# A two-layer graph attention kernel: second layer's tiles cleared earlier in shared memory, transposes three units ahead instead of four, norms over five slots instead of eight

## The chip, the cores and the metric

The kernel runs on one core of one Trainium2 chip. Times are device microseconds of one execution. The engines that appear below are PE (TensorE, matrix products and transposes), PEld (its weight loads), DVE (VectorE), ACT (ScalarE), POOL (GpSimd, which here also issues the gathers), SP (SyncE, which issues most of the other transfers).

## The reference

Two graph attention layers over the same graph, then a norm, the residual and a second norm. B = 8 batches, N = 2048 nodes, 64 channels, H = 4 heads in the first layer and one in the second.

```python
mask = graph + jnp.eye(N, dtype=graph.dtype) > 0
h = jnp.einsum('bnc,hdc->bhnd', x, Wh)
out_h = _gat_layer(h, mask[None, None], bh[None, :, None, :])   # softmax(mask(h h^T)) h + b
z = jax.nn.leaky_relu(cat, negative_slope=0.2)                  # cat: the heads side by side
h2 = jnp.einsum('bnk,dk->bnd', z, Wo)
out2 = _gat_layer(h2, mask[None], bo)
z2 = jax.nn.leaky_relu(out2, negative_slope=0.2)
out = (z2 - mu) * jax.lax.rsqrt(var + LN_EPS) * gamma + beta
x = _layernorm(x + out, axis=-1)
```

The graph is sparse and its first nodes have many neighbours.

## The kernel before

**Hubs and sets.** The first 56 nodes (hubs) are attended densely. The other 1992 nodes form NS = 166 sets of 12. For each set the kernel finds up to 128 nodes that any member is linked to, gathers their rows by an indirect transfer from a table in device memory (`gather`, L792, issued by POOL, some 266 KB each), and computes the attention of the 12 members over these 128 rows for all batches at once.

**First layer.** A loop over i from -4 to 85 works on one pair of sets per turn (NG = 83 pairs), software-pipelined: in one turn the scores of pair i + 1, the values of pair i, the projection of pair i - 1 (`project`, L531), the maps into the second layer of pair i - 2 (`second_maps`, L880) and the rows for the second table of pair i - 3 (`second_rows`, L890; `keep_rows`, L894, and its two stores, L897). Tiles of PSUM have the tags "S" (scores), "C" (`cat`), "O" and "T", one buffer of two banks each; `cat` holds the columns, the projection, the maps and the rows of a turn. The memory of the `early` pool is given back when the loop ends.

**Second layer.** It gathers from the second table, which must be complete. Units are u = 0 to 41, of four sets each (NU = 42; the last has two). The loop runs from u = -4 to 48. Turn u of it issues, in this order:

1. `scores2(u + 2)` (L1133 on PE, exponent L1136 on ACT);
2. `values2(u)` (L1165); an odd unit completes a block of 8 sets in PSUM (tag "O", one buffer) and starts its norm;
3. on some turns `hub_values2` (L1299) for the hub block that began two turns earlier, and the load of a later block (`hub_block`, L1267, issued by SP);
4. the four gathers of unit u + 6;
5. the norm's jobs of this turn's first slot (`work_on(u, 0)`), then `roots` (L1239, L1240 on ACT);
6. `hub_lift2` of the hub block of the turn before (L1285 on DVE, L1288 on ACT);
7. `spread_own(u + 3)` (L1124 on ACT): the members' own columns, copied block-diagonally into one of three `bd` tiles, which `scores2` uses as weights;
8. `turn_scores(u + 1)` (L1144 on PE) and `keep_scores(u + 1)` (L1152 on DVE), which masks the exponents into `es2`, the weights of `values2`;
9. `turn2(u + 4)`: 16 transposes of gathered rows (L512 on PE) and two copies to `xTg` (L1320 on ACT);
10. `hub_scores2` (L1277 on PE);
11. the norm's jobs of the second slot (`work_on(u, 1)`).

The transposes and the hub's scores share the PSUM tag "T" with two buffers. There are 18 hub blocks: four in turns -4 to -1, the others in turns 2, 4, ..., 28.

**The norm** of a block of 8 sets is a list of jobs, spread over turns: `first` (reciprocals L1186 and product L1188), `act` (L1193), `mean` (L1197), `centre` (L1202 on DVE and the square L1204 on ACT), `var` (L1213), `again` (L1217, L1221, L1222: scale, gamma, residual row `xr`), a second `mean`, `centre` and `var`, and `end` (scale L1217 and eight stores L1248). Each turn's list has a part for slot 0 and a part for slot 1:

```python
return [([], [first, act, mean(0)]), ([centre(0)], []), ([var(0)], []), ([], [again, mean(1)]), ([centre(1)], []),
        ([], []), ([var(1)], []), ([end], [])]
```

A new block starts every second turn, so the lists of several blocks overlap. The inverse roots of two variances that fall on one turn are computed together.

**What sets the order.** The schedule is by hand: each engine executes its instructions in the order of the code. Waits between engines come from the tiles: reads after writes, and writes into a tile or buffer after its last reader.

Before the loop of the second layer, and after the first has ended, the code clears `ownb`, `bd`, `es2` and the ends of `esh` (L1107 to L1115), fills `linked` from `mask` (L1117), loads four hub blocks and spreads the first unit.

Of the kernel before, what the change touches and what calls it, by code (L numbers as in the profile page):

```python
# [30 lines left out]
F32 = mybir.dt.float32  # L31
# [13 lines left out]
HUB = 56  # L45
# [314 lines left out]
def fast_kernel(ctx: ExitStack, tc: tile.TileContext, x, adj, Wh, bh, Wo, bo, gamma, beta, out, flag):  # L360
# [53 lines left out]
    nc.vector.tensor_copy(identb, ident)  # L414
    wnat = early.tile([P, H, C], F32, name="wnat")
    whT = early.tile([P, H * D], F32, name="whT")
    gram = early.tile([P, H, P], F32, name="gram")
    wos = early.tile([D, H * D], F32, name="wos")
    woT = early.tile([P, HP, D], F32, name="woT")
# [64 lines left out]
    for k in range(SET):  # L484
        nc.gpsimd.affine_select(out=d, in_=d, pattern=[[0, 3], [-1, 10]], base=-10 * k, channel_multiplier=1,
                                compare_op=OP.not_equal, fill=float(1 << k))
    number = early.tile([P, 2, HALFN], U16, name="number")
    nc.gpsimd.iota(number, [[1, 2], [2, SEG // 2], [SEG, HALFN // (SEG // 2)]], base=0, channel_multiplier=0)
# [20 lines left out]
    def turn(tp, rows):  # L509

        for q in range(Q):
            nc.tensor.transpose(tp[:, q * P:(q + 1) * P], rows[:, q, 1:1 + P], ident)  # L512

# [54 lines left out]

    yh = early.tile([P, 2, 2 * HUB * H], F32, name="yh")

# [91 lines left out]

    keys = [early.tile([P, HALFN], F32, name=f"keys{k}") for k in range(2)]
    cand = early.tile([P, SEG * KEEP], F32, name="cand")
    best = early.tile([P, P], F32, name="best")
    ahead = {}
# [225 lines left out]
    def keep_rows(g, pr):  # L892
        r = rowts[g % 4]
        nc.vector.tensor_tensor(r[:GM, 1:1 + P], pr, bob[:GM].rearrange("n p d -> n (p d)"), OP.add)  # L894
        dst = table2[HUB:, :].rearrange("(n s) (q c) -> s q n c", s=NS, q=Q)
        for j in range(2):
            nc.sync.dma_start(out=dst[2 * g + j], in_=r[j * 48:(j + 1) * 48])  # L897

# [108 lines left out]
    def one(name, tag):  # L1007
        return psum1.tile([P, 2, 512], F32, tag=tag, name=name)

    def late_two(name):  # L1010
        return one(name, "T")

    picks = pick(1)
    ready, done = FIRST, 2 * FIRST
    todo3 = [(10, 0), (14, 1)]
    slow = hub_later(0, one) + hub_later(1, one)
    for i in range(-4, NG + 3):
# [4 lines left out]
        if i >= 1 and slow and len(slow) % 3:  # L1022
            slow.pop(0)()
        cat = one(f"cat{i}", "C")
        if 0 <= i - 1 < NG:
# [14 lines left out]
        if i + 6 < NG and i % 2 == 0 and i >= -2:  # L1040
            own_rows((i + 6) // 2)
        if 0 <= (i - 30) // 2 <= NV:
            (add_beta if i % 2 else load_own)((i - 30) // 2)
# [17 lines left out]
        if 0 <= i - 2 < NG:  # L1061
            second_maps(i - 2, cat[:, 0, 384:384 + GM])
        if 0 <= i - 3 < NG:
            second_rows(i - 3, cat[:GM, 1, 384:512])
        if 0 <= i + 4 < NG + NG % 2:
            columns(i + 4, cat)
        if 0 <= i - 2 < NG:
            keep_own(i - 2, cat[:, 0, 384:384 + GM])
        if 0 <= i - 3 < NG:
            keep_rows(i - 3, cat[:GM, 1, 384:512])  # L1070
        for _ in range((2 if i < 22 or i % 2 else 1) if i >= 0 else 0):
# [10 lines left out]
        if 0 <= i + 3 < NG:  # L1082
            turn(tp[:, 1, :], rows[1, 2 * (i + 3) + 1])
    assert not picks and not pieces and not todo3 and done == NS
    begin.close()
# [11 lines left out]

    NU = (NS + 3) // 4
    sets = [list(range(4 * u, min(4 * u + 4, NS))) for u in range(NU)]
    for u in range(6):  # L1100
        for s in sets[u]:
            gather(table2, s, 2, rows2)
    bd = [late.tile([P, 4, Q, 32], F32, name=f"bd{k}", bufs=1) for k in range(3)]
    es2 = [late.tile([P, 2 * Q, 4, 32], F32, name=f"es2_{k}", bufs=1) for k in range(2)]
    esh = [late.tile([P, Q * 2 * HUB + 8], F32, name=f"esh{k}", bufs=1) for k in range(2)]
    ownb = late.tile([P, Q, 2, HUB], F32, name="ownb", bufs=1)
    nc.vector.memset(ownb, 0.0)  # L1107
    for p in range(2):
        nc.vector.tensor_copy(ownb[half(p), :, p, :], ownh[half(p)].rearrange("c t (k n) -> c (t k) n", k=2))
    for t in bd:  # L1110
        nc.vector.memset(t, 0.0)
    for k in range(2):
        nc.vector.memset(esh[k][:, Q * 2 * HUB:], 1.0)
        nc.vector.memset(es2[k], 0.0)
    nc.vector.memset(es2[0][:, :, :, 24:], 1.0)  # L1115
    linked = late.tile([P, NS, SET], U8, name="linked", bufs=1)
    nc.vector.tensor_scalar(linked, mask.rearrange("p s (k h) -> p s k h", h=H)[:, :, :, 0], 0.0, None, OP.is_equal)  # L1117

    def spread_own(u):

        w = len(sets[u])
        for p in range(2):
            src = own[half(p), :, sets[u][0] * SET:(sets[u][0] + w) * SET]
            nc.scalar.copy(bd[u % 3][half(p), :w, :, 16 * p:16 * p + SET], src.rearrange("c q (k n) -> c k q n", k=w))  # L1124

# [45 lines left out]
    def norm(name, v, i, vals, dens, nb, store):  # L1171

        y = late.tile([P, 8, D], F32, tag="y", name=f"y_{name}", bufs=6)[:, :nb]
        st = late.tile([P, 2, 8], F32, tag="st", name=f"st_{name}", bufs=6)[:, :, :nb]
        at = [v + 2, v + 6]
        xr = late.tile([P, 8, D], F32, tag="xr", name=f"xr_{name}", bufs=3)
# [47 lines left out]
        def end():  # L1224
            scale(1)
            store(y)

        return [([], [first, act, mean(0)]), ([centre(0)], []), ([var(0)], []), ([], [again, mean(1)]), ([centre(1)], []),
                ([], []), ([var(1)], []), ([end], [])]

# [11 lines left out]
    def norm_sets(v, op):  # L1242
        def store(y):
            for t in range(4):
                for a in range(2):
                    dst, w = nodes(t, v)(out, a)
                    p0 = t * 32 + a * SET
                    (nc.scalar if v == NV - 1 and a else nc.sync).dma_start(out=dst, in_=y[p0:p0 + SET].rearrange("p (f w) c -> p f (w c)", f=2)[:, :, :w * D])  # L1248

        view = op[:, :, :4 * W2].rearrange("p f (w c) -> p f w c", w=4)  # L1250
        return norm(f"s{v}", 2 * v + 1, v, view[:, :, :, 1:1 + D], view, 8, store)
# [9 lines left out]

    def hub_block(b):
        t = rows["h", b] = late.tile([P, Q, PW], F32, tag="hrows", name=f"gh{b}", bufs=4)
        n = HUB if b == NHB else hub_sets(b)[1] * SET
        s0 = b * S10
        src = table2[:HUB, :] if b == NHB else table2[HUB:, :].rearrange("(k s) c -> s k c", s=NS)[s0:s0 + n // SET]
        nc.sync.dma_start(out=t.rearrange("n q c -> n (q c)")[:n], in_=src)  # L1267

# [35 lines left out]
    def spread(u, parts):  # L1304

        for k, part in enumerate(parts):
            for t in range(2):
                jobs.setdefault((u + k, t), []).extend(part[t])

# [4 lines left out]
    def turn2(u):  # L1314
        for g in sorted({s // 2 for s in sets[u]}):
            tp = bank2(f"t2_{g}", "T", 2)
            for j in range(2):
                turn(tp[:, j, :], rows[2, 2 * g + j])
            t = held["T", 2, g] = late.tile([P, 2, 512], F32, tag="xTg", name=f"xTg2_{g}", bufs=6)
            nc.scalar.copy(t, tp)  # L1320
# [24 lines left out]

    hub_at = {u: b for b, u in enumerate([-4, -3, -2, -1] + list(range(2, 2 * NHB, 2))[:NHB - 3])}
    assert len(hub_at) == NHB + 1
    for b in range(4):
        hub_block(b)
    spread_own(0)  # L1350
    for u in range(-4, NU + 7):
        if 0 <= u + 2 < NU:
            scores2(u + 2)
        if 0 <= u < NU:
            a = u % 2
            if a == 0:
                op = bank2(f"o2_{u}", "O")
            values2(op, sets[u], es2[a], a, len(sets[u + 1]) if a == 0 else 0)
            if a == 1:
                spread(u, norm_sets(u // 2, op))  # L1360
        if u - 2 in hub_at:
            b = hub_at[u - 2]
            hub_values2(b, b == 0, b == NHB)
            if b + 4 <= NHB:
                hub_block(b + 4)
            if b == NHB:
                spread(u, norm_hub(u, oh2))
        for s in sets[u + 6] if 0 <= u < NU - 6 else []:
            gather(table2, s, 2, rows2)
        work_on(u, 0)  # L1370
        roots(u)
        if u - 1 in hub_at:
            hub_lift2(hub_at[u - 1])
        if 0 <= u + 3 < NU and u > -3:
            spread_own(u + 3)
        if 0 <= u + 1 < NU:
            turn_scores(u + 1)
            a = (u + 1) % 2
            if u + 3 == NU and len(sets[NU - 1]) < 4:

                nc.vector.memset(es2[a][:, :, len(sets[NU - 1]):, SET:2 * SET], 1.0)
            keep_scores(u + 1, a)
        if u + 4 < NU:
            turn2(u + 4)
        if u in hub_at:
            hub_scores2(hub_at[u])
        work_on(u, 1)
        if u == -3:
            range_of(0, rall)
            lists_fit()  # L1390
        if u == NU - 1:
            range_of(1, rall2)
            in_limits()
# [40 lines left out]
```

## Time and profile before

| | us |
|---|---|
| median of three runs | 1047.05 (1044.12 to 1052.09) |
| the profiled execution | 880.76 |
| its span | 878.9 |
| mean granted PE clock in it | 0.951 |

| engine | busy us | share of the span |
|---|---|---|
| PE | 753.0 | 86% |
| PEld | 661.2 | 75% |
| DVE | 610.1 | 69% |
| ACT | 514.4 | 59% |
| POOL | 469.2 | 53% |

Durations below are from the profiled execution, which was shorter than the timed runs. "Idle before <-X" in a row is the time an engine did nothing ahead of an instruction, and what ended it. "issue" is time with no visible cause. An engine's share over the whole span mixes three stages: up to about 600 us the first layer, from there to about 850 us the second, then a tail of norms and stores.

### The profile page before, as it was taken

The page shows a single profiled execution, that of the slowest core. Times are in us where ns is not written, and L with a number is a line of the kernel's source. Part 1 is how long each engine was busy: PE and PEld are TensorE (multiplying, and loading weights), DVE is VectorE, ACT ScalarE, POOL GpSimd, SP SyncE. Part 2 cuts the span into 40 slices and gives each one's busy share as a digit, 9 for nine tenths or more (in the row PEclk, how much of TensorE's full clock was granted, in tenths as well). Part 3 has the DMA queues.
Part 4 walks back from the last instruction along what each step waited for, and adds up shares of the span by engine and source line. Part 5 has one row for each costly group of instructions (what it writes and reads, how often), then busy time and mean ns, then how long its engine had stood idle before and what let it go on. Part 6 is the DMA issues. An engine that isn't in the chain of part 4 may idle for free.

```text
span 878.9 us, 42066 instructions
## 1 busy us (share of the span) xinstructions
PE 753.0 (86%) x18437; PEld 661.2 (75%) x18437; DVE 610.1 (69%) x1369; ACT 514.4 (59%) x961; POOL 469.2 (53%) x612
## 2 busy tenths in 40 slices
PE   1896777889999999999999999992999999998730
PEld 1664456778788999988999999971899999988720
DVE  3356983568888788877555555553258999998994
ACT  2342333556556667666766667651678888886821
POOL 5654141457444555655666666503777777777300
PEclk9998998999999999999999999995999999999965
DMA  8787451355434445655566665514888888888611
GB/s 167 238 218 213 129 146 48 83 142 160 109 100 118 112 125 159 162 169 153 160 168 173 160 166 162 134 28 114 246 266 253 275 275 267 266 252 242 172 46 35
DMA packets 81794, 145.22 MB, mean 165 GB/s; under 512 B 30146, under 2 KB 46466, under 8 KB 81602
## 3 DMA queue, kind: packets, MB, share of 16 engines
q0 software_dynamic: 26720, 88.55, 36.4%
q1 hardware_dynamic: 37842, 49.65, 18.7%
q10 hardware_dynamic: 17040, 4.25, 2.6%
q8 instruction: 147, 2.41, 1.1%
q14 instruction: 45, 0.37, 0.1%
HBM read 123.91 MB, written 18.48 MB: 162 GB/s over the span
## 4 chain that ended last, share of the span: by engine, by line
PE 63%; DVE 15%; DMA 7%; ACT 5%; issue 4%; SPq 3%; POOL 2%; DVEq 0%; ACTq 0%; POOLq 0%
PE t L512 11%; PE s L821 10%; PE o L846 10%; PE cat L806 6%; PE o L863 4%; PE cat L531 4%; PE cat L880 3%; PE s L1133 3%; PE o L1165 3%; PE cat L890 2%; DMA raw<-in_adj_dram 2%; SPq L1248 2%; PE sh L1277 2%; PE e L1144 2%; DMA g<-table,index 1%
## 5 line engine op out<-in xcount | busy, mean ns | idle before, releaser
L792 POOL DMA_INDIRECT g<-table,index x332 | 334.9, 1009 | 236.1 <-PE o L846 140.2
L512 PE MATMUL t<-ident,g 128*128 128x128 f32 x1328 | 182.3, 276 | 15.6 <-DMA g<-table,index 12.7
L512 PEld LDWEIGHTS t<-ident,g 128*128 128x128 f32 x1328 | 154.8, 142 | 20.0 <-issue 14.0
L826 DVE TENSOR_TENSOR e<-s,mask 128x768 f32<-128x768 f32 x83 | 79.4, 956 | 87.4 <-PE s L821 85.4
L518 ACT ACTIVATE z<-cat,bhp 128x192 f32<-128x192 f32 x166 | 60.8, 418 | 85.0 <-PE cat L531 85.0
L846 PE MATMUL o<-g,e 128*64 128x65 f32 x2656 | 97.5, 227 | 0.0
L821 PEld LDWEIGHTS s<-y,xTg 64*64 64x64 f32 x5312 | 85.2, 134 | 13.9 <-issue 13.7
L821 PE MATMUL s<-y,xTg 64*64 64x48 f32 x5312 | 95.5, 220 | 0.0
L846 PEld LDWEIGHTS o<-g,e 128*64 128x64 f32 x2656 | 85.8, 140 | 9.8
L1320 ACT COPY xTg<-t 128x1024 f32<-128x1024 f32 x83 | 80.3, 1017 | 18.1 <-PE t L512 17.3
L1030 ACT COPY xTg<-t 128x1024 f32<-128x1024 f32 x83 | 84.0, 1012 | 2.0 <-PE t L512 2.0
L833 ACT ACTIVATE e<-e,shifts 128x768 f32<-128x768 f32 x83 | 79.2, 955 | 2.1 <-DVE e L826 1.7
L812 ACT COPY y<-cat 128x384 f32<-128x384 f32 (+1 forms) x80 | 40.7, 508 | 64.0 <-PE o L863 40.1
L597 ACT ACTIVATE e<-e,shifts 128x896 f32<-128x896 f32 x32 | 33.4, 1042 | 73.0 <-DVE e L594 52.1
L680 POOL TENSOR_SCALAR a<-raw 120x1024 bf16<-120x1024 int32 (+1 forms) x34 | 38.2, 1125 | 65.1 <-DMA raw<-in_adj_dram 38.4
L806 PE MATMUL cat<-xo,gram 128*128 128x192 f32 (+1 forms) x320 | 65.6, 328 | 0.0
L853 DVE RECIPROCAL rall<-o 64x8 f32<-64x8 f32 x166 | 34.0, 205 | 42.0 <-PE o L846 40.7
L854 DVE TENSOR_TENSOR osb<-o,rall 128x512 f32<-128x512 f32 x83 | 57.4, 692 | 2.9
L1165 PE MATMUL o<-g,es 128*32 128x65 f32 x2656 | 49.1, 226 | 5.9 <-DVE y_s L1188 4.5
L806 PEld LDWEIGHTS cat<-xo,gram 128*128 128x128 f32 x320 | 53.7, 203 | 0.3 <-issue 0.2
L1165 PEld LDWEIGHTS o<-g,es 128*32 128x32 f32 x2656 | 46.1, 113 | 7.0 <-issue 4.9
L1133 PE MATMUL s<-xTg,bd 128*32 128x128 f32 x1328 | 45.4, 277 | 6.2 <-ACT bd L1124 3.5
(177 smaller groups left out, 1369.3 us busy)
## 6 DMA issues: line engine op xcount, KB each, us to landing
raw<-in_adj_dram SPq DMA_DIRECT2D x32, 480.0 KB
table<-xb SPq DMA_DIRECT2D x22, 256.0 KB
xr_s<-table SPq DMA_DIRECT2D x21, 256.0 KB
g<-table,index POOLq DMA_INDIRECT x332
table<-x SPq DMA_DIRECT2D x16, 260.0 KB
x<-in_x_dram ACTq DMA_DIRECT2D x32, 128.0 KB
table<-rowt SPq DMA_DIRECT2D x166, 24.4 KB
xb<-in_x_dram SPq DMA_DIRECT2D x164, 24.0 KB
```

Of the source, the lines that this page charges most:

```text
L512: nc.tensor.transpose(tp[:, q * P:(q + 1) * P], rows[:, q, 1:1 + P], ident)
L518: nc.scalar.activation(z[:, hp], cat[:, :, hp * n:(hp + 1) * n], AF.Identity, bias=bhp[:, hp:hp + 1], scale=1.0)
L792: nc.gpsimd.indirect_dma_start(out=t.rearrange("n q c -> n (q c)"), out_offset=None, in_=table, in_offset=bass.IndirectOffsetOnAxis(ap=ind ...
L806: nc.tensor.matmul(cat[:, k, 2 * GM:2 * GM + n], gram[:, g % 2 * 2 + k, :], held["x", g // 2][:, :n], start=True, stop=True)
L821: nc.tensor.matmul(sp[half(r), p, (q * 2 + j) * M:(q * 2 + j + 1) * M], xt[half(p), j, q, half(r)], y[half(p), (j * Q + q) * M:(j * Q + q ...
L826: nc.vector.tensor_tensor(e[:, :16 * M].rearrange("p (a q n) -> p a q n", a=2, q=Q), sp[:, :, :8 * M].rearrange("p a (q n) -> p a q n", q= ...
L833: nc.scalar.activation(e[:, :16 * M], e[:, :16 * M], AF.Exp, bias=shifts[:, 0:1], scale=1.0)
L846: nc.tensor.matmul(op[half(p), j, o0:o0 + K1], e[:, c0:c0 + 64], rw[j][:, q, sums(p)], start=True, stop=True)
L1030: nc.scalar.copy(t, held.pop(("tp", i + 2)))
L1133: nc.tensor.matmul(sp[q * 32:(q + 1) * 32, k, :], bd[u % 3][:, k, q, :], xt[:, s % 2, q, :], start=True, stop=True, tile_position=(0, q * 32))
L1165: nc.tensor.matmul(op[t * 32:(t + 1) * 32, f, k * W2 + p:k * W2 + p + K1], e[:, 2 * q + p, k, :], rw[:, q, sums(p)], start=(a == 0 and k = ...
L1320: nc.scalar.copy(t, tp)
```

## The change

- The tiles that the second layer clears are no longer allocated at its start. They are views of six tiles `share` in the pool that lives throughout, whose memory first serves helpers of the first layer (`wnat`, `wos`, `number`, `yh`, `keys`, `cand`, `best`). `linked` lies in a part of `maskh`. The clears, `linked` and the first three `spread_own` become eleven jobs, one in every second turn of the first layer's loop from i = 61.
- In the first layer's last turns the maps and the rows have PSUM tiles of their own (from i = 83), and no `cat` is allocated after that turn. In the last two pairs the second store of rows is issued by ACT.
- `turn2` is three units ahead instead of four, and stands right after the norm's first slot. The loop starts at -3. The hub blocks start at turns -3, -2, -1, 2, 4, ..., 30. The first four hub loads wait for transposes of the first units.
- The norm takes five turns instead of eight, `first` ahead of the other jobs of its slot. `roots` comes at the end of the turn. The stores of the last block go over SP, ACT and POOL.

```diff
+    bd = [t.rearrange("p (k q n) -> p k q n", k=4, q=Q) for t in (share[2][:, :512], share[2][:, 512:], share[4])]
+    es2 = [t.rearrange("p (b k n) -> p b k n", b=2 * Q, k=4) for t in share[:2]]
+    ahead_of_second = ([clear_own] + [lambda t=t: nc.vector.memset(t, 0.0) for t in bd + es2] + [clear_ends, link] +
+                       [lambda u=u: spread_own(u) for u in range(3)])
...
-        cat = one(f"cat{i}", "C")
+        cat = one(f"cat{i}", "C") if i <= NG else None
+        if i < NG:
+            ph, pr = cat[:, 0, 384:384 + GM], cat[:GM, 1, 384:512]
+        else:
+            ph, pr = one(f"ph{i}", "S")[:, 0, :GM], one(f"pr{i}", "T")[:GM, 0, :P]
...
+        if i >= 60 and i % 2 and ahead_of_second:
+            ahead_of_second.pop(0)()
...
-            nc.sync.dma_start(out=dst[2 * g + j], in_=r[j * 48:(j + 1) * 48])
+            (nc.scalar if j and g >= NG - 2 else nc.sync).dma_start(out=dst[2 * g + j], in_=r[j * 48:(j + 1) * 48])
...
-        return [([], [first, act, mean(0)]), ([centre(0)], []), ([var(0)], []), ([], [again, mean(1)]), ([centre(1)], []),
-                ([], []), ([var(1)], []), ([end], [])]
+        return [([first], [act]), ([mean(0), centre(0)], [var(0)]), ([again], [mean(1)]), ([centre(1)], [var(1)]), ([], [end])]
...
-                jobs.setdefault((u + k, t), []).extend(part[t])
+                now = jobs.setdefault((u + k, t), [])
+                now[:] = now + part[t] if k else part[t] + now
...
-    for u in range(-4, NU + 7):
+    for u in range(-3, NU + 5):
         if 0 <= u + 2 < NU:
             scores2(u + 2)
         if 0 <= u < NU:
...
+        for s in sets[u + 6] if 0 <= u < NU - 6 else []:
+            gather(table2, s, 2, rows2)
+        work_on(u, 0)
+        if u + 3 < NU:
+            turn2(u + 3)
+        if u in (-3, -2):
+            for k in range(2):
+                hub_block(2 * (u + 3) + k, held["at", 4 * (u + 3) + 2 * k + 1])
         if u - 2 in hub_at:
             b = hub_at[u - 2]
             hub_values2(b, b == 0, b == NHB)
             if b + 4 <= NHB:
                 hub_block(b + 4)
             if b == NHB:
-                spread(u, norm_hub(u, oh2))
-        for s in sets[u + 6] if 0 <= u < NU - 6 else []:
-            gather(table2, s, 2, rows2)
-        work_on(u, 0)
-        roots(u)
+                spread(u + 2, norm_hub(u + 2, oh2))
         if u - 1 in hub_at:
             hub_lift2(hub_at[u - 1])
-        if 0 <= u + 3 < NU and u > -3:
+        if 3 <= u + 3 < NU and u >= 0:
             spread_own(u + 3)
         if 0 <= u + 1 < NU:
             turn_scores(u + 1)
...
-        if u + 4 < NU:
-            turn2(u + 4)
         if u in hub_at:
             hub_scores2(hub_at[u])
         work_on(u, 1)
+        roots(u)
```

The rest moves the definitions up and changes the turns of the final checks (`range_of`) by one.

## The prediction

> **What bounds the kernel now.** I read the engine totals first, then busy time by stretch, then the timeline of one pair of units of the second layer, then the seam between the layers and the tail.
>
> Busy time by stretch (columns: stretch, length, busy and count for PE, PEld, DVE, ACT, POOL, then granted clock, DMA share, GB/s):
>
> ```profile
> 600.00:651.00 51.00, 36.84 (x693) 32.83 (x694) 17.66 (x37) 25.65 (x42) 34.85 (x36) 0.82 0.77 231
> 651.00:788.00 137.00, 134.01 (x3334) 123.94 (x3333) 124.25 (x221) 111.66 (x195) 105.31 (x105) 1.00 0.87 261
> 788.00:850.00 62.00, 45.41 (x1225) 40.68 (x1223) 57.28 (x107) 39.61 (x74) 27.82 (x27) 0.92 0.61 175
> 850.00:879.00 29.00, 0.19 (x2) 0.09 (x2) 16.44 (x32) 4.40 (x12) 0.00 (x0) 0.50 0.15 34
> ```
>
> In the second layer's steady stretch (651 to 788) PE is nearly solid, but DVE is 91% busy and ACT 82%: nobody has room. From 788 on DVE leads; the last 29 us have no PE work.
>
> The timeline of one pair (start, length, engine, line, idle before it). An odd unit begins with its value product at 711.74, the next odd unit at 722.25: period 10.51 us.
>
> ```profile
> 711.74 1.13 PE L1165 MATMUL o<-g,es 128*32 128x65 f32 x64
> ...
> 713.50 0.56 DVE L1152 TENSOR_TENSOR es<-e,linked 128x384 f32<-128x384 f32 x1
> 713.61 0.67 ACT L1288 ACTIVATE esh<-esh,shifts 120x448 f32<-120x448 f32 x1
> 713.97 0.41 DVE L1186 RECIPROCAL rall<-o 64x8 f32<-64x8 f32 x2
> 714.18 0.70 ACT L1124 COPY bd<-own 64x192 f32<-64x192 f32 x2
> ...
> 714.90 1.93 ACT L1320 COPY xTg<-t 128x1024 f32<-128x1024 f32 x2
> 715.14 0.81 PEld L1133 LDWEIGHTS s<-xTg,bd 128*32 128x32 f32 x32 [0.17 <-issue]
> ...
> 717.79 0.63 ACT L1204 ACTIVATE sq_s<-y_s 128x512 f32<-128x512 f32 x1 [0.24 <-DVE y_s L1202]
> ...
> 720.34 1.09 PE L1277 MATMUL sh<-ownb,own 128*120 128x112 f32 x8 [0.23 <-ACT xTg L1320]
> ```
>
> What to see: the scores (L1133) start at 715.14, while the copies of this unit's transposes (L1320) have only just begun. Those copies feed the scores one unit later. This whole unit of slack is why PE loses just 0.23 us a pair although ACT, whose instructions here stand in the order of the code, also waits for DVE (0.24 before the square).
>
> The seam and the tail:
>
> ```profile
> 599.94 0.42 PE L890 MATMUL cat<-ident,own 128*96 128x128 f32 x1 [0.70 <-DVE rowt L894]
> ...
> 605.05 0.43 DVE L1107 MEMSET ownb<- 128x448 f32 x1 [4.36 <-DMA table<-rowt]
> 605.49 0.96 POOL L792 DMA_INDIRECT g<-table,index  x1 [5.56 <-DVE ownb L1107]
> ```
> ```profile
> 633.26 1.09 PE L1165 MATMUL o<-g,es 128*32 128x65 f32 x64
> ```
> ```profile
> 867.92 7.03 SPq L1248 DMA_DIRECT2D out_dram<-y_s  x11
> ```
>
> The first gather goes 5.5 us after the first layer's last product, gathers then follow every 1.25 us (605.49, 606.76, 608.01), and the first value product comes at 633.26, held back by the fourth unit's transposes, that is by the 16th gather. At the end SP still issues stores until 874.95, 0.64 us each, though DVE ended at 869.43.
>
> [...]
>
> **The change, part by part.** The sum is made against the profiled execution, 880.76 us (span 878.9). The median, 1047.05, is 166 us above it; I return to this.
>
> 1. *Clears and block-diagonal copies moved into the first layer.* Eleven jobs, one in every second unit from i = 61: one clear with two copies (0.43 + 0.57), three clears of 0.52, two of 0.91, 0.4 of small ones, `linked` 1.20, three `spread_own` of 0.70 on ACT. The units are 5.00 us long there; DVE shows 1.61 us idle before L826 in each, ACT 0.66 and 0.93. The DVE job delays the copy of `rowt` (530.21 to 530.49 in a unit whose next `cat` product starts at 531.85): slack 1.3 us, the longest job 1.2. I take nothing; without this cover all of it, 6 us of DVE and 2 of ACT, is the upper end. Nothing can be gained within those units.
>
> 2. *Seam.* With `ph` and `pr` in banks of their own, the maps of the last unit no longer wait for `rowt` (597.95 becomes about 597.0, when L523 ends); the last `rowt` ends near 598.8 for 600.69. ACT takes every second store of the last two units, one SP issue of 0.59 each. The gather also no longer sits behind the late pool's clear (605.05 to 605.49). First gather near 602.7: 2.8 us earlier. Transposing three units ahead, the first value product needs the 12th gather and not the 16th: 4 x 1.25 = 5 us. Together **-8** (-5 if half of the seam stays; -10 with the hub loads out of the gathers' way, since SP now issues them after transposes; nothing else is behind them in SP's queue before the first `xr` load).
>
> 3. *Steady state.* No instruction is added, but the order is. Now transposes for u+3 are turned in unit u and needed by the scores at the start of unit u+1: the slack unit is gone. ACT's copies stand behind the squares, and `bd` behind the copies. On DVE an odd unit now has `first` (which waits for this unit's value product) and `again` ahead of the hub subtraction and `keep_scores`; an even unit has `centre(1)`, `mean(0)`, `centre(0)` ahead. The loop, from the start of an odd value product as 0, with starts as they follow each other in the pair above:
>  - DVE: `first` from 1.15 (L1186 0.45, L1188 0.73) to 2.33; `again` 3 x 0.72 to 4.5; hub subtraction 0.54 to 5.05; `keep_scores` 0.47 to 5.5; `act` 0.73, `end` 0.60, `mean(1)` 0.60, `centre(1)` 0.60, `mean(0)` 0.60, `centre(0)` 0.68: 9.33.
>  - ACT: square to 10.0, two copies 1.93 to 11.93, `bd` 0.70 to 12.63.
>  - PE: scores from 12.65, next odd value product 0.89 later: **13.54**, against 10.51.
>
>  Within it, the even unit's scores wait too: hub subtraction 5.1, exponent 0.67, `bd` 0.70: 6.45, where they began at 3.40 before. PE idles about 2 us there and is done with the even unit's transposes at 10.2, ahead of ACT, so the loop above stays the longest. In odd units the hub's score tile still holds one of the two "T" banks, so the second transposes wait for the first copy, about 1.1 us, inside the same idle time. Fifteen periods (odd units 3 to 33) are 15 x 13.54 = 203. After the hub blocks a period is 13.0 (no subtraction); three of them 39; the last, without transposes, 9.6; the hub's norm, some 5 us of small DVE operations, falls into this part: 54. Sum 257. Before, L1188 runs from 651.29 to 851.25: 200.0 for the same 19 periods. **+57**. Bounds: +25 if ACT's squares stand in the way but half of DVE's order overlaps, +70 if odd and even stalls add.
>
> 4. *Drain.* From the last L1186 (850.80) DVE took 18.6 us; in five slots, by the same durations, 17. The stores of the unit before the last now leave some 5 us earlier, the last eight go over three queues: about 2 us of issues for 5.5. **-5.5** (0 to -8).
>
> Sum: 880.8 - 8 + 57 - 5.5 = **924** in the profiled execution, +5%.
>
> *To the median.* The page does not show why the timed runs take 166 us more. If it is a lower PE clock, 753 us of PE work at 0.951 would have to run at about 0.79 (an estimate). Then a pair needs 10.28/0.79 = 13 us of PE before, and in the changed order about 15.4 (the even unit's 5.9 us of PE becomes 7.5 and follows a start at 7.9); 15 x 2.35 + 10 after the hub blocks - 14 = +31. If it is a constant, +43. I take 1047 + 35 = **1082**.
>
> **The rivals.**
> - *The loop does not bind* (ends on the other side). PE's 134 of 137 us and an unchanged number of instructions speak for it: the pair would stay at 10.5, and seam and drain give -13.5: 1033. It needs the DVE-ACT loop to be 3 us shorter than the walk, for example `again` overlapping PE entirely. Against: DVE has 0.64 us idle in a pair and is in order. From a loop below 11.2 us the change gains (0.7 x 19 = 13).
> - *Half of it*: only the even unit's wait for `bd` costs, period 11.2 to 11.5: +13 to +19 against -13.5: 1050.
> - *POOL becomes the pace*: eight gathers of 1.25 are 10.0 us a pair, below 10.5, so it can hold back the early units only; then the seam gains 3 and not 8 while the loop stands: 1087.
> - *The change does not do what it says*: the clears are not covered and the drain stays: 8 + 5.5 more, 1096.
>
> **How the numbers follow.** 0.72 for the loop (1058 to 1112 with the bounds and the last two rivals), 0.12 for half of it (1040 to 1057), 0.16 for no loop (1025 to 1039). A measurement of this kernel tells about 1% from no change. Faster 0.15, within 1% 0.11, slower 0.74. The range 1040 to 1112 leaves out the no-loop case and the far ends of the first.
>
> **What would show it.** Right: in the steady part L1188 to L1188 of neighbouring pairs near 13.5 us; PE's scores L1133 waiting for ACT (`bd` or `xTg`) in both units; ACT's square waiting for DVE, over 1 us; PE's busy share there near 75%; first value product near 625; last DVE to end some 5 us. Wrong: a period at or below 11, or PE waiting in the first layer from i = 61 on.

## The result and the profile after

| | before | after | ratio after to before |
|---|---|---|---|
| first measurement, median of 4 runs each | 1045.59 us | 1108.43 us | 1.0594 [1.0557, 1.0631] |
| both again, medians | 1045.66 us | 1107.86 us | 1.0592 [1.0509, 1.0676] |

The change makes the kernel 5.9% slower. The prediction was 1082 us, with 1040 to 1112 as its range and 0.74 on slower.

The absolute times need one sentence ahead of all that follows: the runs came from several chips, on two of them the kernel before takes 1040 to 1046 us and on two others 881 or 882 us, and the profile of before shown above is like the latter. Where it matters the chip is therefore named by the time of before on it, and runs are compared by their ratio to before on the same chip. The ratio hardly depends on it: 1.0605 [1.0485, 1.0724] for (nearly) the kernel after on a chip of the quick kind.

The engine totals of after, and the shares of its chain of waits (columns as above):

```profile
PE 846.5 (76%) x18437; PEld 719.5 (65%) x18437; DVE 612.9 (55%) x1369; ACT 518.5 (47%) x959; POOL 465.6 (42%) x614
...
PE 58%; DVE 13%; another core or an unknown queue 10%; ACT 8%; issue 5%; DMA 3%; POOL 2%; SPq 0%; ACTq 0%; DVEq 0%; POOLq 0%
```

DVE and ACT do what they did, in a longer span. A tenth of the chain ends on something that the trace does not name. Busy time by stretch, cut where the stages of before were cut (seam, second layer, its end, tail):

```profile
638.00:690.00 52.00, 25.99 (x286) 20.20 (x287) 4.48 (x10) 9.43 (x12) 25.86 (x28) 0.66 0.56 160
690.00:1010.00 320.00, 214.51 (x3948) 178.99 (x3947) 139.91 (x247) 132.08 (x229) 119.30 (x124) 0.82 0.50 135
1010.00:1084.00 74.00, 47.42 (x985) 41.27 (x986) 49.23 (x95) 34.28 (x64) 14.67 (x15) 0.81 0.34 92
1084.00:1110.50 26.50, 1.27 (x34) 0.92 (x34) 15.48 (x30) 3.77 (x10) 1.23 (x2) 0.50 0.16 36
```

In the second layer PE is busy 67% of the time (214.51 of 320), DVE 44%, ACT 41%, and the granted clock is 0.82: nobody is the limit, they wait for each other.

The profile of before that is fit to set beside it is one from the same chip. Both kernels were therefore profiled once more on the chip where before takes 1045.66 us (`b_again`, `a_again`). Cut by the starts of named products (last scores of the first layer, L823; first and last value product of the second, L1180; L821 and L1165 in before), and likewise for the quick chips:

| stage, us | before | after | difference | before, quick chip | after, quick chip (`e4_pad128`) | difference | forecast |
|---|---|---|---|---|---|---|---|
| start to last scores | 613.5 | 619.6 | +6.1 | 584.8 | 589.5 | +4.7 | 0 |
| seam, to the first value product | 66.5 | 62.1 | -4.4 | 48.4 | 39.4 | -9.0 | -8 |
| first to last value product | 320.8 | 398.7 | +77.9 | 213.1 | 274.2 | +61.1 | +57 |
| drain, to the end | 32.3 | 26.2 | -6.1 | 32.5 | 26.8 | -5.7 | -5.5 |
| span | 1033.2 | 1106.6 | +73.4 | 878.9 | 929.9 | +51.0 | +43.5 |

The time is lost in the steady part of the second layer, as forecast; two stages give some back. (The profiled execution of `b_again` took 1035.14 us, 11 less than its median, so the differences on this chip are too large by about as much. The forecast's +57 was made for a stretch that is cut a little differently, from the second block's L1188 to the last one's.)

### The profile page after: what moved, and what is told of

The parts are those of the page before. It is cut to its first block, busy times and chain, and to the rows that moved or that the text cites. A ratio compares the mean times of both kernels' runs of the same rounds, so it can differ in the third digit from the quotient of the medians.

```text
span 1110.5 us, 42062 instructions
## 1 busy us (share of the span) xinstructions
PE 846.5 (76%) x18437; PEld 719.5 (65%) x18437; DVE 612.9 (55%) x1369; ACT 518.5 (47%) x959; POOL 465.6 (42%) x614
## 3 DMA queue, kind: packets, MB, share of 16 engines
q8 instruction: 147, 2.41, 0.9%
## 4 chain that ended last, share of the span: by engine, by line
PE 58%; DVE 13%; another core or an unknown queue 10%; ACT 8%; issue 5%; DMA 3%; POOL 2%; SPq 0%; ACTq 0%; DVEq 0%; POOLq 0%
PE t L513 12%; PE s L823 9%; PE o L848 8%; PE cat L808 4%; PE s L1148 4%; ACT xTg L1340 3%; PE cat L533 3%; PE o L865 3%; PE o L1180 3%; PE e L1159 3%; PE cat L882 2%; PE cat L892 2%; DVE var L1228 2%; DVE e L596 1%
## 5 line engine op out<-in xcount | busy, mean ns | idle before, releaser
L513 PE MATMUL t<-ident,g 128*128 128x128 f32 x1328 | 217.5, 295 | 89.2 <-ACT xTg L1340 56.7
L513 PEld LDWEIGHTS t<-ident,g 128*128 128x128 f32 x1328 | 165.4, 151 | 116.3 <-ACT xTg L1340 60.1
L823 PE MATMUL s<-y,xTg 64*64 64x48 f32 x5312 | 115.1, 222 | 6.4 <-issue 5.7
L823 PEld LDWEIGHTS s<-y,xTg 64*64 64x64 f32 x5312 | 98.8, 134 | 26.4 <-issue 18.5
L1148 PE MATMUL s<-xTg,share 128*32 128x128 f32 x1328 | 61.2, 342 | 58.1 <-ACT share L1028 48.8
L1148 PEld LDWEIGHTS s<-xTg,share 128*32 128x32 f32 x1328 | 44.7, 136 | 71.1 <-ACT share L1028 62.0
L1167 DVE TENSOR_TENSOR share<-e,maskh 128x384 f32<-128x384 f32 (+1 forms) x42 | 23.1, 549 | 116.6 <-PE e L1159 95.5
L1180 PE MATMUL o<-g,share 128*32 128x65 f32 x2656 | 62.4, 264 | 4.4 <-DVE share L1167 4.2
L1180 PEld LDWEIGHTS o<-g,share 128*32 128x32 f32 x2656 | 59.9, 141 | 5.9 <-DVE share L1167 4.8
L1201 DVE RECIPROCAL rall<-o 64x8 f32<-64x8 f32 x42 | 8.6, 205 | 95.9 <-remote 79.6
```

The lines of the kernel that those rows point to most:

```text
L513: at = nc.tensor.transpose(tp[:, q * P:(q + 1) * P], rows[:, q, 1:1 + P], ident)
L823: nc.tensor.matmul(sp[half(r), p, (q * 2 + j) * M:(q * 2 + j + 1) * M], xt[half(p), j, q, half(r)], y[half(p), (j * Q + q) * M:(j * Q + q ...
L1148: nc.tensor.matmul(sp[q * 32:(q + 1) * 32, k, :], bd[u % 3][:, k, q, :], xt[:, s % 2, q, :], start=True, stop=True, tile_position=(0, q * 32))
L1180: nc.tensor.matmul(op[t * 32:(t + 1) * 32, f, k * W2 + p:k * W2 + p + K1], e[:, 2 * q + p, k, :], rw[:, q, sums(p)], start=(a == 0 and k = ...
```

## The experiments

Theory **L** is that of the prediction: PE, ACT and DVE wait for each other in a loop of 13.54 us per pair of units. Two parts of the change are in it: the transposes three units ahead and the norm over five slots (four units long) with its new order.

### Twice the same, and PE's instructions shifted

Because the pair takes about 20.75 us on the chip of the first measurement, not 13.5, a rival was needed at once: **F**, that PE's own instructions come late there. `b_again` and `a_again` are the two kernels unchanged.

> The kernel before, unchanged, profiled once more, because its timed runs (1042 to 1052 us) lie 165 us above its profiled execution (880.8). Theory L (the longer loop of DVE and ACT): a pair of units takes 10.5 us in the profile and the 165 us are a lower PE clock spread over the kernel. Theory F (PE's instruction stream arrives late): the profile shows either about 880 us again with no stall, or about 1045 us with stalls of some 4 us on PE that no semaphore explains, each beginning near a transfer of the instruction queue.

> The changed kernel, unchanged, profiled once more on the same chip. Theory L: pairs of 13.5 us in undisturbed stretches. Theory F: again pairs near 20.8 us, with one stall of 4 us a pair in the odd unit just after its first eight transposes, and near 1108 us in all, so the stall belongs to the kernel and not to one execution.

Measured: 0.999 of before, and 1.0592. For `b_again` neither theory was met cleanly: before, too, has pairs of 14 to 18 us on this chip, but its granted clock is 0.936, and its longer stops are mostly of 1.9 to 3.3 us from one product to the next, about one a pair. `a_again` is what F expected: pairs of 20 to 21 us, 15 stops of 3.7 to 4.2 us after the odd unit's first eight transposes, and 1107.86 us in all; no pair of its steady part is near the 13.5 us of L. One such stop (timeline: start, length, engine, line, idle before it and its releaser):

```profile
856.60 1.41 PE L513 MATMUL t<-ident,g 128*128 128x128 f32 x8
...
860.67 0.42 DVE L1201 RECIPROCAL rall<-o 64x8 f32<-64x8 f32 x2 [5.15 <-remote]
860.76 1.01 ACT L1340 COPY xTg<-t 128x1024 f32<-128x1024 f32 x1 [4.07 <-remote]
860.90 0.94 POOL L794 DMA_INDIRECT g<-table,index  x1 [1.17 <-remote]
...
861.83 1.50 PE L513 MATMUL t<-ident,g 128*128 128x128 f32 x7 [3.82 <-ACT xTg L1340]
```

The value product on which L1201 waits began at 855.58 and takes 1.1 us. Even so, DVE, ACT and POOL all start within 0.25 us of each other, DVE 5.1 us after that product's start, where 1.5 is the normal distance (`e4_pad128` below), as if PE's signals had come in a bunch. A 16 KB transfer of the instruction queue (one of 147, 2.41 MB) lies at 857.87; in `before` 25 of them begin from 651 to 788 us, about two a pair. That the transfer brings PE's instructions, or causes the stop, is not shown. In `a_again` each of the 15 stops begins within 1.9 us of the start of a transfer, but in `b_again` all but one of the stops ahead of the hub's scores begin 3 to 4.5 us away from one.

F supposes, as the author's guess, that PE's instructions come in these transfers and that the stops stand where one ends. `e4_pad128` would move such borders against the second layer's loop, with 32 one-column products ahead of it (128 more PE instructions in the record, weight loads included), and leaves the rest of after as it is.

```diff
+    pad = bank2("pad", "T", 2)
+    for _ in range(32):
+        nc.tensor.matmul(pad[0:1, 0, 0:1], ones, ones, start=True, stop=True)
```

> The changed kernel with 32 products of one column each ahead of the second layer's loop, into a bank that nobody reads, while PE waits for the first gathers. [...] Theory L: within 1% of the changed kernel (1097 to 1118). Theory F (half of the loss is where PE's instruction blocks end in a unit): the pair changes by more than 1.5 us, the total by more than 25 us either way.

Measured: 934.0 us against 882.14, ratio 1.0605 [1.0485, 1.0724], on a quick chip. There PE does not stop so: its second transposes start after 1.10 us of idle time, for 3.82 in the fence above. In `before`, whose profile is like those of the quick chips, PE is never idle for more than 0.24 us at a time from 651 to 788 us, for all of the 25 transfers there. So F can't be judged by this run. But it shows the loop undisturbed, and the pair is 13.55 us. From its timeline:

```profile
714.01 1.09 PE L1180 MATMUL o<-g,share 128*32 128x65 f32 x64
...
715.49 0.42 DVE L1201 RECIPROCAL rall<-o 64x8 f32<-64x8 f32 x2 [1.58 <-PE o L1180]
...
718.61 0.61 DVE L1304 TENSOR_TENSOR share<-sh,maskt 120x448 f32<-120x448 f32 x1
719.14 0.55 DVE L1167 TENSOR_TENSOR share<-e,maskh 128x384 f32<-128x384 f32 x1
...
720.59 1.08 PE L1148 MATMUL s<-xTg,share 128*32 128x128 f32 x32 [1.83 <-ACT share L1028]
...
722.84 0.69 DVE L1217 SCALAR_TENSOR_TENSOR y_s<-st_s,y_s 128x512 f32<-128x512 f32 x1
...
723.57 0.63 ACT L1219 ACTIVATE sq_s<-y_s 128x512 f32<-128x512 f32 x1 [0.62 <-DVE y_s L1217]
724.10 1.91 ACT L1340 COPY xTg<-t 128x1024 f32<-128x1024 f32 x2
...
725.90 0.71 ACT L1028 COPY share<-own 64x192 f32<-64x192 f32 x2
...
726.66 1.08 PE L1148 MATMUL s<-xTg,share 128*32 128x128 f32 x32 [0.16 <-ACT share L1028]
...
727.56 1.09 PE L1180 MATMUL o<-g,share 128*32 128x65 f32 x64
```

Read it from the top as the walk of the prediction: value product, `first`, then `again` until the hub subtraction at 718.61 (4.60 after the start; forecast 4.5), `keep_scores` at 5.13 (5.05), last `centre` at 8.83 (8.65), square at 9.56 (9.33), copies, `bd`, scores at 12.65 (12.65), next odd value product at 13.55 (13.54). Halfway, the even unit's scores wait 1.83 us for `bd`, which stands behind the hub exponent (start at 6.58; forecast 6.45).

### One part undone at a time

`e1_four5` keeps the new norm and gives the slack unit back:

```diff
+    turn2(0)
     for u in range(-3, NU + 5):
...
-        if u + 3 < NU:
-            turn2(u + 3)
...
+        if u + 4 < NU:
+            turn2(u + 4)
         if u in hub_at:
             hub_scores2(hub_at[u])
```

> The changed kernel with the transposes four units ahead again, at their old place at the end of a unit; norms over five slots, early clears and spread stores stay. Theory L (the loss is the loop of DVE and ACT that the missing unit of slack closes): the copies leave the loop, a pair falls from 20.8 to about 17, the total to 1050 to 1062. Theory N (the loss is the norm's order alone): 1095 to 1108. Theory B (the loss is the second pair of transposes that waits for the first copy while the hub's scores hold a bank): as in L, but below 1045.

`e2_three8` keeps the transposes three ahead and gives the norm its eight slots and their old order back; `e3_four8` undoes both, and keeps the early clears, the seam, the hub loads and the spread stores.

```diff
-        return [([first], [act]), ([mean(0), centre(0)], [var(0)]), ([again], [mean(1)]), ([centre(1)], [var(1)]), ([], [end])]
+        return [([], [first, act, mean(0)]), ([centre(0)], []), ([var(0)], []), ([], [again, mean(1)]), ([centre(1)], []),
+                ([], []), ([var(1)], []), ([end], [])]
```

> The changed kernel with the norm over eight slots in the old order; transposes stay three units ahead. Theory L: the squares and the work of DVE no longer stand ahead of the copies, but the copies still feed the next unit's scores: a pair about 18.5, total 1065 to 1080. Theory N: 1038 to 1048. Theory B: the bank is held as in the changed kernel, 1095 to 1110.

> The changed kernel with both undone: what is left are the early clears in shared memory, the seam with its own banks and ACT's stores, the later hub loads and the spread last stores. All theories: pairs as in the kernel before (near 16.8), and the seam's gain of about 4 us less some 3 to 6 us that the first layer lost: 1037 to 1047.

| run (before 882.14 us) | time | ratio | a pair, us |
|---|---|---|---|
| `e1_four5` | 942.8 | 1.0705 [1.0591, 1.0818] | 13.83, about every second one 14.7 to 15.3 |
| `e2_three8` | 959.47 | 1.0894 [1.0782, 1.1005] | 14.2 and 16.4 in turn |
| `e3_four8` | 890.06 | 1.0106 [0.9987, 1.0225] | 10.4 to 11.6 |

The expectations are in times of the chip where before takes 1046 us; as ratios, L meant 1.00 to 1.02 for `e1_four5` and 1.02 to 1.03 for `e2_three8`. For `e1_four5` L and B failed: with the slack unit back the pair is no shorter. N, the norm's order alone, came nearest (1.05 to 1.06); for `e2_three8` N failed as well (it expected 0.99 to 1.00). `e2_three8` is slower than all of its three. `e3_four8` is near what was expected, 1% above before. Undone together, the loss is gone. So each part alone is enough, the two do not add, and L as told (the missing slack unit) is not the whole cause. In `e2_three8` the second transposes and the copies wait for the hub subtraction, which frees their PSUM bank, and `bd` stands behind the copies (PE's scores wait 1.6 to 1.8 us for it once a pair):

```profile
725.20 1.10 PE L513 MATMUL t<-ident,g 128*128 128x128 f32 x8 [1.97 <-DVE share L1305]
...
728.56 1.08 PE L1148 MATMUL s<-xTg,share 128*32 128x128 f32 x32 [1.83 <-ACT share L1028]
```

In `e1_four5` a second loop of nearly the same length appeared: in the odd unit through `first`, `again`, the hub subtraction and what follows it to the next unit's value product, 7.47 us, and then 6.36 us of PE's own work for the even unit:

```profile
718.52 0.62 DVE L1304 TENSOR_TENSOR share<-sh,maskt 120x448 f32<-120x448 f32 x1
...
719.20 1.09 PE L513 MATMUL t<-ident,g 128*128 128x128 f32 x8 [2.72 <-DVE share L1304]
...
720.50 1.08 PE L1148 MATMUL s<-xTg,share 128*32 128x128 f32 x32 [0.21 <-ACT share L1028]
```

`e3_four8` also shows the clears. They run from pair 61 on, so I take the time from the scores of pair 50 to those of pair 82: 159.6 us in before, 166.4 in `e3_four8`, and 165.9 to 166.9 in each of the kernels with the clears in the loop on the quick chips. One of the eleven jobs in the timeline of `e3_four8`:

```profile
490.12 2.13 DVE L1033 COPY share<-ownh 64x224 f32<-64x224 f32 x2
...
490.81 1.29 POOL L930 TENSOR_TENSOR xb<-xb,bet 128x512 f32<-128x512 f32 x1
...
493.29 0.50 ACT L814 COPY y<-cat 128x384 f32<-128x384 f32 x1 [3.42 <-DVE rowt L896]
...
494.27 0.92 PE L533 MATMUL cat<-otb,whT 64*64 64x96 f32 x16 [2.29 <-ACT otb L872]
```

DVE's two copies for `ownb` take 2.13 us here. They delay `rowt`, `rowt` holds `cat`, ACT's copy of the next `cat` starts after 3.42 us of idle time, and PE waits 2.29 us. The unit lasts 9.0 us and not 5.0 (7.5 in `e4_pad128`).

### Where on DVE the delay stands

If `e1_four5` is held by the hub subtraction behind `again`, the subtraction and its exponent put ahead of the norm's first batch must free it. `e5_four5_lift` does that to `e1_four5`, `e6_three5_lift` to after.

```diff
+        if u - 1 in hub_at:
+            hub_lift2(hub_at[u - 1])
         work_on(u, 0)
...
-        if u - 1 in hub_at:
-            hub_lift2(hub_at[u - 1])
```

> The kernel after with the transposes four ahead again (as in e1_four5), and with the hub mask subtraction and its exponent put ahead of the unit's first batch of norm jobs, so ahead of `again`. Theory two loops (e1 stayed slow because first, again, hub subtraction, second transposes and bd copy make a loop of their own of about 7.5 us in the odd unit): that loop loses some 3 us, a pair takes 10.8 to 12.3 us instead of 13.8, and the time is 1.01 to 1.04 of before. Rival (what holds is that keep_scores stands behind `again`): a pair stays at 13 to 14 and the time at 1.055 to 1.075.

> The kernel after, with only the hub mask subtraction and its exponent put ahead of the unit's first batch of norm jobs. Theory two loops: the loop through square, copies, bd and scores is left whole but for the subtraction, so a pair is 12.8 to 13.6 us and the time 1.045 to 1.06 of before. Rival (the hub exponent behind `again` is the one cause, the loop that was forecast only a coincidence of numbers): a pair falls to 10.5 to 11.5 and the time to 1.00 to 1.02.

Measured, before 880.82: `e5_four5_lift` 922.06 us, 1.0475 [1.0425, 1.0525], pair 13.27; `e6_three5_lift` 928.29 us, 1.0522 [1.0480, 1.0564], pair 13.02. The second loop was not freed: the rival on `keep_scores` was right on the pair of `e5_four5_lift`, though its time lies between the two expectations. `e6_three5_lift` is within what the two loops meant. What PE's scores wait for has changed, first in `e5_four5_lift`, then in `e6_three5_lift`:

```profile
717.13 0.55 DVE L1167 TENSOR_TENSOR share<-e,maskh 128x384 f32<-128x384 f32 x1
...
717.83 1.08 PE L1148 MATMUL s<-xTg,share 128*32 128x128 f32 x32 [1.86 <-DVE share L1167]
```
```profile
719.69 0.55 DVE L1167 TENSOR_TENSOR share<-e,maskh 128x384 f32<-128x384 f32 x1
...
720.39 1.08 PE L1148 MATMUL s<-xTg,share 128*32 128x128 f32 x32 [1.87 <-DVE share L1167]
```

Scores and their transposition share one PSUM tile (tag `S2`, one buffer). So the scores of a unit can't start before `keep_scores` has read that tile, and `keep_scores` stands behind `first` and `again` just as the hub subtraction did. Taking one victim out of the queue shows the next. The size of the loop through the square is confirmed as well: without the subtraction it should be 13.0, and `e6_three5_lift` has 13.02.

`e9_four5_last` therefore puts the norm's first batch behind all of them, directly ahead of the second batch, in `e1_four5`:

```diff
-        work_on(u, 0)
...
         if u in hub_at:
             hub_scores2(hub_at[u])
+        work_on(u, 0)
         work_on(u, 1)
```

> e1_four5 (transposes four ahead, four-unit norm) with one edit: the unit's first batch of norm jobs (first, again, and in the other unit mean and centre) stands directly ahead of its second batch, so behind the hub subtraction, keep_scores, the transposition of the scores and the copies. Theory (what costs is only that `again` and its like stand ahead of the hub subtraction and keep_scores on VectorE and their squares ahead of the copies on ScalarE; the length of the norm in units is innocent): a pair takes 10.4 to 11.2 us instead of 13.8, and the time is 1.00 to 1.02 of before, its rest above 1 being the clears in the first layer. Rival (four units in place of eight put too many VectorE steps in one unit, so that the norm's length itself holds the pair): a pair stays at 12.5 to 14 and the time at 1.04 to 1.07.

Measured, on a chip where before takes 1039.83: 1057.8 us, 1.0162 [1.0116, 1.0208]. The ratio is the theory's. Its pair is not, because the expectation is in times of a quick chip: 17.5 to 18.6 us, where `b_again` has about 17 and `a_again` about 20.75. First to last value product are 344.6 us, against 320.8 and 398.7, so 54 of the 77.9 us are gone with the norm still in five slots. From `a_again` two things differ, the slack unit and the moved line; since `e1_four5`, on a quick chip, had the slack unit and lost as much as after, most of it is put down to the line, across two kinds of chip. The waits of PE from 760 to 960 us (line, releaser: us in total, times, longest), in `e9_four5_last` and in `b_again`:

```profile
PE sh L1296 <- ACT xTg L1340: 40.6, 11, 3.8
```
```profile
PE sh L1277 <- ACT xTg L1320: 21.8, 10, 3.1
```

What is left, about 1.2 us a pair, is at the hub scores, behind copies that follow a stop of PE. Whether the stop only falls at a worse place or the norm still costs something was not told apart; it needs this kernel on a quick chip, which was not tried.

### The clears elsewhere, and what the change can give

`e7_late_clears` is `e3_four8` with the eleven jobs after the first layer's loop.

```diff
-        if i >= 60 and i % 2 and ahead_of_second:
-            ahead_of_second.pop(0)()
...
+    for job in ahead_of_second:
+        job()
```

> e3_four8 (both second-layer parts undone) with the eleven jobs (clears, link, first three spreads) run in one go after the first layer's loop instead of one every second unit in it. Theory (the jobs delay the first layer by 5 to 7 us and cost nothing in the seam, where VectorE waits): last first-layer scores at 584 to 587 us instead of 592, first value product no later after them than in e3 (44.7) by more than 1 us, time 0.995 to 1.005 of before. Rival (the first layer's 7 us come from somewhere else in the change, the stores' queues or the banks of the last products): last scores stay at 590 to 592 and the time at 1.01.

Measured, before 880.82: 883.25 us, 1.0022 [1.0000, 1.0045]. From pair 50 to pair 82 it takes 160.1 us, against 159.6 in before and 166.4 in `e3_four8`; the last scores are at 587.2. The same two copies, now with POOL idle beside them:

```profile
601.69 0.56 DVE L1033 COPY share<-ownh 64x224 f32<-64x224 f32 x2
```

The seam is 46.2 us, 1.5 more than in `e3_four8` and still 2.2 less than in before. Moving the clears into the first layer thus gained 1.5 us of the seam for some 6 us of the first layer: they fit nearly whole into a seam in which DVE waits.

`e8_best` adds the shorter seam (three ahead up to unit 0, four from there) and the five-slot norm for the last two blocks alone:

```diff
+        if u <= 0:
+            turn2(u + 3)
...
-        if u + 4 < NU:
+        if 0 <= u < NU - 4:
             turn2(u + 4)
...
+        short = NV - 2 <= i < NV
+        at = [v + 1, v + 3] if short else [v + 2, v + 6]
```

> e7_late_clears with the two gains of the change kept and its two losses left out: transposes three ahead until unit 0 (shorter seam) and four ahead from there on, the four-unit norm for the last two blocks alone. Theory: seam 4 to 5 us shorter than e7, drain 5 to 6 us shorter, pairs of the second layer at 10.5 to 11: 0.982 to 0.994 of before. Rival (the short order holds the last four units as it held the others, and the start at unit 0 has to make up a whole transposition): 0.997 to 1.005.

Measured: 882.34 us, 1.0017 [0.9993, 1.0041]. The rival's time was right. The profiled execution took 888.7 us, 6 more than the median, so only its two ends are read here. The seam is 40.5 us, 5.7 less than in `e7_late_clears` (4 to 5 expected), but the drain is 31.8, not 26 to 27. DVE's busy time from the last value product to its last operation, in before, `e4_pad128` and `e8_best` (columns as in the stretches above, DVE is the third):

```profile
846.00:869.50 23.50, 1.28 (x34) 0.94 (x34) 20.34 (x38) 4.91 (x13) 0.00 (x0) 0.50 0.19 42
```
```profile
903.00:920.70 17.70, 1.28 (x34) 0.94 (x34) 15.62 (x31) 3.90 (x10) 0.00 (x0) 0.50 0.17 40
```
```profile
855.00:877.20 22.20, 1.28 (x34) 0.94 (x34) 20.10 (x39) 5.78 (x17) 0.00 (x0) 0.50 0.19 42
```

The drain is DVE's: 20.1 of 22.2 us busy. In `e8_best` these windows hold 39 operations of DVE, as in before (38), in `e4_pad128` 31, 4.7 us less. The five slots for the last two blocks alone shorten nothing; that DVE is then still working off the blocks before them is an argument.

`e10_all_last` joins `e9_four5_last`, the late clears and the seam of `e8_best`:

```diff
-    turn2(0)
     for u in range(-3, NU + 5):
...
+        if u <= 0:
+            turn2(u + 3)
...
-        if u + 4 < NU:
+        if 0 <= u < NU - 4:
             turn2(u + 4)
```

> e9_four5_last with the clears run after the first layer's loop and the transposes three ahead up to unit 0. Theory: the first layer as in e7, the seam about 40.5 us as in e8, a pair 10.4 to 11.2, and the drain, where VectorE only works off what stands behind it, 26 to 30 us instead of 32: 0.983 to 0.997 of before. Rival (the short drain of the change came from the pair's long waits, in which VectorE caught up; with pairs at 10.5 us the same work stands behind the last products): drain 31 to 32 us and 0.995 to 1.004.

Measured, before 1039.83: 1053.87 us, 1.0121 [1.0086, 1.0157], above both expectations. Against `b_again`: pair 50 to pair 82 171.2 us, for 171.0; seam 61.5, 5.1 less; drain 28.5, 3.8 less, within what the theory said of it and not the rival's 31 to 32; but first to last value product 347.1, 26.3 more, with the same waits as in `e9_four5_last`. No version beat the kernel before by more than the intervals.

All runs together say what shortens the drain. Counted strictly from the start of the last value product, the kernels with eight slots, and `e8_best`, have 36 or 37 DVE operations behind it and drains of 31.8 to 32.5 us. Those with five slots throughout have 29 to 32, and 26.2 to 28.7 us. Long pairs are not enough: `e2_three8` has pairs of 14.2 to 16.4 us and `b_again` of about 17, and both drain in 32.3 us.

## Why the prediction was right, and where it was not

The time, 1108.43 us, lies inside the range, 4 us from its upper end and 26 above the number. The loop was forecast rightly. That the total still fits is in part luck, since two terms, the clears and the step to the median, were too small.

- **The loop.** Right in mechanism and size: 13.54 us a pair forecast, 13.55 measured in `e4_pad128`, each station within 0.35 us. For the stretch of the forecast, from the second block's L1188 (L1203 in after) to the last one's, 257 was forecast and 256.5 measured in `e4_pad128` (648.28 to 904.73), against 200.0 in before; from the first to the last value product it is +61.1. PE's busy share from 648 to 840 us is 77% (75 forecast), but the square waits 0.62 us and not over 1. On the chip of `a_again` the pair takes about 20.75 us for about 16.8 in `b_again`, so the excess is 3.9 and not 3.0.
- **Its cause.** "The slack unit is gone" was one of two sufficient causes. The other is the order on DVE: `e1_four5` has the slack unit and loses as much, and `e9_four5_last`, with only the order changed from there, loses a quarter of that by the ratio (1.0162 for 1.0705, on another kind of chip). The prediction named both but walked a single loop; it did not see that `keep_scores` holds the scores' PSUM tile.
- **The "T" bank.** 1.1 us of wait inside the idle time forecast; the second transposes in `e4_pad128` wait 1.10 us, and in this kernel the wait decides nothing. With only one part undone it does: PE's second transposes wait 2.72 us for the bank in `e1_four5` and 1.97 in `e2_three8` (fences above).
- **Clears at nothing.** This failed, and the prediction's own sign for it, PE waiting in the first layer from i = 61 on, came true. The term "slack 1.3 us, the longest job 1.2" was mis-sized twice: the first job alone took 2.56 us (0.43 and the 2.13 shown), and the smaller ones also lengthened their units, by 0.25 (clears of 512), 0.76 (of 1024) and 0.85 us (`linked`) in `e3_four8`. Cost from pair 50 to pair 82: 6.3 to 7.3 us on the quick chips, 5.0 where before takes 1046 (`a_again` 176.0, `b_again` 171.0), close to the upper end of 6 + 2.
- **Seam and drain.** -8 and -5.5 forecast, -9.0 and -5.7 measured on a quick chip, -4.4 and -6.1 on the other. The seam's parts held on the quick chip: the first gather comes 3.4 us earlier after the last scores (2.8 forecast), the first value product another 5.6 us earlier after that gather (5 forecast). The drain's number was right by luck. Mainly the queues were charged, and DVE's last operation was to lie some 5 us before the end; it lies 9.2 us before it, for 9.4 in before. What shrank is DVE's work behind the last product: it ends 17.5 us after that product's start, for 23.1 in before.
- **To the median.** The 35 us added here failed; the difference is 62.8. It was worked out as a lower PE clock or a constant. Neither holds. The clock would have had to be about 0.79 (the working gives 0.78), but `b_again` shows 0.936, for 0.951 in the profile of before. Of the 154 us that its span is longer, PE is idle for 82 more, and its products take 72 more by the record, where their ends are modelled. A constant would have given the same difference on both kinds of chip, but by the medians it is 62.2 us there and 51.9 for `e4_pad128`. That the new waits cost no clock was the author's guess; it held on the quick chip (1.00 in `e4_pad128` from 648 to 840 us), not on the other (0.82 in `a_again` from 710 to 1060, 0.95 in `b_again` from 705 to 985). Simply carrying the ratio over would have been nearer: 924/880.8 is 1.049, and 1047 times that is 1098.
- **The rivals.** That the loop does not bind, or only half of it (11.2 to 11.5 us), is excluded by the period. POOL as the pace: PE never waits for a gather in the pair shown, and the seam gained 9.0 us on the quick chip, not 3. The clears not covered did happen, as half of the last rival; its other half, the undiminished drain, did not.

## What to carry to other kernels

ACT and DVE kept to the order of the code in these traces: in `before` ACT's square waited 0.24 us, until 717.79, and the copies of `bd`, which do not need it, went after it, at 718.33; in `e4_pad128` DVE's hub subtraction came at 718.61, behind `again`, though no product for its scores (L1296) ran from 713.90 on. Moving a batch of work forward in such an order costs whatever now stands behind it, and taking one victim out of the queue only uncovers the next: list everything that the batch overtakes, the readers that free a PSUM tile among it. The drain shortened here only where fewer operations stood behind the last product, and a wait that is already idle (here the seam) was a better place for clears than a loop without slack. When the profile and the timed runs differ by a sixth, the ratio is the better guess than the difference.

## What the runs showed of the hardware

- The same kernel takes 881 to 882 us on two chips and 1040 to 1046 on two others. The loss is PE's: DVE is busy for 610.1 us in `before` and 612.8 in `b_again`, ACT for 514.4 and 518.3, PE for 753.0 and 825.2, with 82 us more of idle time. In the fence of `a_again` DVE, ACT and POOL start within 0.25 us of each other, 5.1 us after the start of PE's product. Why stays open; that PE's instructions come late is a suspicion that no run settles.
- DVE's pair of copies took 2.13 us in the first layer's loop (`e3_four8`) and 0.56 us after it (`e7_late_clears`); in the first case a POOL addition of 1.29 us runs beside it. Only the second copy is long, 1.84 us for 0.27, and nearly the same in all nine traces that have the copies in the loop. It begins 0.40 us ahead of the addition and ends some 0.15 us after it. Beside a gather's issue on POOL of 0.96 us, in `before`, the two copies take 0.57 us. No run took the POOL addition away from beside the copies in the loop, so whether it lengthens the copy is not shown.
